# Layer 0's softmax sums: from a spread matmul and four wide reciprocals to a round trip through DRAM

## The chip, the cores and the metric

The kernel runs on one core of a Trainium2 chip, as one launch. The metric is the device time of that launch in microseconds (us); three runs of the kernel before gave 4754.49 to 4755.42 us, with a median of 4754.79 us.

## What is computed

Two attention layers run one after the other on `x` of shape (2, 256, 64, 64): two images, 256 channels, 4096 positions each. Layer 0, cut to what matters here:

```python
# xn: x normalised over its channels; q, k, v: 4 heads of 16 each
attn = softmax(einsum('bhnd,bhmd->bhnm', q, k) * SCALE, axis=-1)
d1   = relu(conv1_w @ x + conv1_b)
dyn  = conv2_w @ d1 + conv2_b            # one number for each position n
attn = attn * dyn[:, :, :, None]
out  = einsum('bhnm,bhmd->bhnd', attn, v)
x    = sigmoid(gamma * (out_w @ out) + x)
```

The kernel does not divide the 4096x4096 weights of a head by their sum. It gathers the unnormalised exponentials times v, and the sum of the exponentials beside it, and multiplies the gathered result by dyn / sum at the end. That factor, one number for each head and position, is what the change is about. Layer 1 is an ordinary attention of 4 heads of 64 with a projection and a residual; the change does not touch its code.

## The kernel before, in words

**Units and steps.** Layer 0's attention is cut into 16 units, one for each image and block of 512 query positions (`units0`). A unit runs 32 steps (`NM`), one for each 128 key positions. In every step and for each of the 4 heads, `weigh` makes the scores of those 128 keys against the 512 queries on TensorE (L440) and their exponentials on ScalarE (L443). One step later `gather` adds exponentials times v into one PSUM bank (L455): each head has a strip of 32 rows, and the first row of the strip is the sum of the exponentials, because the first column of v is one.

A second stream runs beside this and about one unit ahead (`LEAD0`, 35 steps): `maxima` makes scores of a later unit on TensorE (L402), and VectorE takes their maximum over the keys (L406), for the shift of the exponentials. A step is made of two halves, and each half emits on TensorE two score matmuls, two matmuls for maxima, and half of a gather (columns 0 to 255, then 256 to 511).

**Around the end of a unit.** When the last gather of a unit is done, ScalarE copies its bank to SBUF (`avs`, L469). What follows is hung into the steps of the next unit by `at(step, place, ...)`. With t0 the first step of the unit and NM = 32:

- `sums` at t0+33 "end": a matmul with the 0/1 matrix `spread` (L482) repeats each head's sum row over the 32 rows of its strip, in one of four PSUM banks that it shares with the maxima;
- `keep_sums` at t0+34 "start": ScalarE copies that bank to the tile `f` (L488);
- `invert` at t0+35 to t0+38 "middle": VectorE inverts `f` in four pieces of 128 columns (L492), the same number 32 times over;
- `scale` at t0+38 "end": GpSimd multiplies `f` by `dyn`, which was loaded with every row the same (L477), and then `avs` by `f` (L496, L497);
- `project` at t0+41 and t0+43 "end": TensorE multiplies by the output weights, 128 channels at a time (L502); `add_x` half a step later on VectorE adds the residual (L507);
- `finish` at t0+45 "end": a tanh on ScalarE (L516), a scaling on GpSimd (L517), and the store of the layer's output `x1` (L518).

**What sets the order.** Compute instructions are wrapped in `seq`, so that each engine runs them in the order in which the code emits them. DMAs are not: nearly all of them go to SyncE's queue (SP), and the framework places them in it, often well before the step that emits them. That queue is worked off in order, and a DMA that waits holds up what stands behind it. PSUM tiles rotate: the maxima, sums, projections and shifts share four banks (`bank`), the scores have three (`ps2`), the gather one (`psa`). A matmul waits until the earlier reader of its bank is done.

**The last unit.** From 35 steps before the end no maxima are left. The last unit runs beside layer 1's first projections (L618, L651) and the loads of their inputs, and part of its scores goes to the four shared banks.

Of the kernel before, what the change touches and what calls it, by code (L numbers as in the profile page):

```python
# [8 lines left out]
F32 = mybir.dt.float32  # L9
BF16 = mybir.dt.bfloat16  # L10
AF = mybir.ActivationFunctionType
ALU = mybir.AluOpType
# [3 lines left out]
P = 128  # L16
NB = 512
C = 256
CC = C // P
H = 4  # L20
# [7 lines left out]
def conv_attention_kernel(  # L28
# [19 lines left out]
    nc = tc.nc  # L48
    B, _, N = x.shape
    NJ = N // NB  # L50
    NM = N // P
    PB = NB // P

    const = ctx.enter_context(tc.tile_pool(name="const", bufs=1))
    dram = ctx.enter_context(tc.tile_pool(name="dram", bufs=1, space=bass.MemoryType.DRAM))
    small = ctx.enter_context(tc.tile_pool(name="small", bufs=2))
# [6 lines left out]
    l0w = own0.enter_context(tc.tile_pool(name="l0w", bufs=2))  # L63
# [11 lines left out]
    dyn0 = [  # L75
        [dram.tile([1, NB], F32, tag=f"dyn0_{b}_{j}", name=f"dyn0_{b}_{j}") for j in range(NJ)]
        for b in range(B)
    ]
    x1 = [
        [dram.tile([C, NB], F32, tag=f"x1_{b}_{j}", name=f"x1_{b}_{j}") for j in range(NJ)]  # L80
        for b in range(B)
# [4 lines left out]
    def load_x(b, j, pool=xpool, tag="x"):  # L86
        t = pool.tile([P, CC, NB], F32, tag=tag, name=f"{tag}_{b}_{j}")
        nc.sync.dma_start(
            out=t, in_=x[b, :, bass.ts(j, NB)].rearrange("(c p) n -> p c n", p=P)
        )  # L90
        return t
# [120 lines left out]
    seq = tc.keep_in_program_order  # L212
# [3 lines left out]
    def at(t, place, step):  # L216
        extras.setdefault((t, place), []).append(step)
# [13 lines left out]
    units0 = [(b, j) for b in range(B) for j in range(NJ)]  # L231
# [5 lines left out]
    with own0:  # L237
# [14 lines left out]
        work, qs0, mxs, pts, avs, dyns, res, facts = {}, {}, {}, {}, {}, {}, {}, {}  # L252

        def bank(name):
            return banks[0].tile([P, NB], F32, tag="bank", name=name)
# [129 lines left out]
        def load_q(u):  # L385
            b, j = u
            if u not in qs0:
                q = l0w.tile([P, NB], F32, tag="q", bufs=4, name=f"q_{b}_{j}")
                nc.sync.dma_start(out=q, in_=q0[b][j])
                qs0[u] = q  # L390
# [17 lines left out]
        def fold(u):  # L408
            seq(nc.vector.tensor_reduce(
                negmax0[u[1] % 2].rearrange("p i (h e) -> p (i h) e", e=32)[:, :, 0],  # L410
                mxs.pop(u), AX.X, ALU.max, negate=True,
            ))

        def turn(u):

            ps = bank("nm0_{}_{}".format(*u))
            for i in range(PB):
                seq(nc.tensor.matmul(
                    ps[:, bass.ts(i, P)], negmax0[u[1] % 2][:, i, :], ident,
                    start=True, stop=True,  # L420
                ))
            work["turn"] = ps

        def shift_q(u):
            seq(nc.vector.tensor_add(qs0[u], qs0[u], work.pop("turn")))
# [47 lines left out]
        def load_residual(u):  # L473
            b, j = u
            res[u] = load_x(b, j, res_pool, "res")
            dyns[u] = l0w.tile([P, NB], F32, tag="dyn", bufs=1, name=f"dyn_{b}_{j}")
            nc.sync.dma_start(out=dyns[u], in_=dyn0[b][j].partition_broadcast(P))  # L477

        def sums(u):
            b, j = u  # L480
            ps = bank(f"sums0_{b}_{j}")
            seq(nc.tensor.matmul(ps, spread, avs[u], start=True, stop=True))  # L482
            f = l0w.tile([P, NB], F32, tag="f", bufs=1, name=f"f0_{b}_{j}")
            facts[u] = f, ps

        def keep_sums(u):
            f, ps = facts[u]
            seq(nc.scalar.copy(f, ps))  # L488

        def invert(u, i):  # L490
            f, _ = facts[u]
            seq(nc.vector.reciprocal(f[:, bass.ts(i, P)], f[:, bass.ts(i, P)]))  # L492

        def scale(u):
            f, _ = facts.pop(u)
            seq(nc.gpsimd.tensor_tensor(f, f, dyns.pop(u), ALU.mult))  # L496
            seq(nc.gpsimd.tensor_tensor(avs[u], avs[u], f, ALU.mult))  # L497

        def project(u, c):
            b, j = u  # L500
            ps = bank(f"o0_{b}_{j}_{c}")
            seq(nc.tensor.matmul(ps, wo0[:, bass.ts(c, P)], avs[u], start=True, stop=True))  # L502
            work["o", c] = ps

        def add_x(u, c):
            xt = res[u]
            seq(nc.vector.scalar_tensor_tensor(  # L507
                xt[:, c, :], work.pop(("o", c)), gam, xt[:, c, :], ALU.mult, ALU.add
            ))

        def finish(u):
            b, j = u
            avs.pop(u)
            xt = res.pop(u)

            seq(nc.scalar.activation(xt, xt, AF.Tanh, scale=0.5))  # L516
            seq(nc.gpsimd.tensor_scalar(xt, xt, 0.5, 0.5, ALU.mult, ALU.add))  # L517
            nc.sync.dma_start(out=x1[b][j].rearrange("(c p) n -> p c n", p=P), in_=xt)  # L518


        for n, u in enumerate(units0):
            t0 = n * NM
            at(t0 - LEAD0 - 8, "start", lambda u=u: load_q(u))
            at(t0 - 4, "end", lambda u=u: fold(u))
            at(t0 - 3, "end", lambda u=u: turn(u))
            at(t0 - 2, "start", lambda u=u: shift_q(u))
            at(t0 + 12, "start", lambda u=u: load_residual(u))
            at(t0 + NM + 1, "end", lambda u=u: sums(u))
            at(t0 + NM + 2, "start", lambda u=u: keep_sums(u))
            for i in range(PB):  # L530
                at(t0 + NM + 3 + i, "middle", lambda u=u, i=i: invert(u, i))
            at(t0 + NM + 6, "end", lambda u=u: scale(u))
            for c in range(CC):
                at(t0 + NM + 9 + 2 * c, "end", lambda u=u, c=c: project(u, c))
                at(t0 + NM + 10 + 2 * c, "start", lambda u=u, c=c: add_x(u, c))
            at(t0 + NM + 13, "end", lambda u=u: finish(u))


        blocks = [(b, j) for b in range(B) for j in range(NJ)]
        for n in range(len(blocks) + 3):  # L540

            def block(k):
                return blocks[n - k] if 0 <= n - k < len(blocks) else None
# [7 lines left out]
            new, middle, old = block(0), block(1), block(2)  # L551
# [116 lines left out]
        for i in range(NJ):  # L668
            k = (0, 0, i)
            t1 = T0 + 2 + 2 * i  # L670
# [3 lines left out]
            t1 = T0 + 20 + 3 * i if i < PB else END0 + (2, 3, 4, 9)[i - PB]  # L674
# [49 lines left out]
    with (  # L724
# [330 lines left out]
        for n, u in enumerate(units):  # L1055
            b, g, j = u
            t0 = n * US
# [5 lines left out]
            if n < len(units) - NJ:  # L1063
# [9 lines left out]
                t1 = (n // NJ * NJ + NJ - 1) * US  # L1073
                at(t1 + 2 * j + 2, "start", lambda to=to: load_keys(*to))
                at(t1 + 2 * j + 3 + LAG, "start", lambda to=to: load_values(*to))
            for k in range(NG):
                t1 = t0 + (k + 1) * GS // 2
# [6 lines left out]
            t1 = t0 + US + GS // 2  # L1084
# [8 lines left out]
            if b < B - 1 and (g, j) == (PR - 1, NJ - 1):  # L1093
                for i in range(NJ):
                    t1 = t0 + US + (i + 4) * GS // 2
# [99 lines left out]
        for j in range(NJ):  # L1195
            project_half(j, 1, last_att[0][:, bass.ts(j, NB)])
            nc.sync.dma_start(
                out=out[B - 1, :, bass.ts(j, NB)].rearrange("(c p) n -> p c n", p=P),
                in_=last_x[j],
# [51 lines left out]
```

## Time and profile before

| | |
|---|---|
| median of three runs | 4754.79 us |
| the profiled execution's own time | 4754.21 us |
| its span | 4752.1 us |
| TensorE busy (matmuls) | 4539.4 us, 96% of the span |
| VectorE busy | 3957.7 us, 83% |
| ScalarE busy | 3399.4 us, 72% |
| GpSimd busy | 2554.3 us, 54% |
| the 16 units' results are copied (L469) | first at 343 us, last at 2057 us |
| from one such copy to the next | 115.66 us in the regular units, 95.6 us in the last |

The profile is one execution. A busy share is the share of the span in which an engine had an instruction in flight; an engine at 96% need not set the time everywhere, and an engine at 70% may do so where another waits for it. Layer 0's attention ends at about 2070 us; the rest is layer 1.

### The profile page before, as it was taken

How to read it: one execution, taken by the hardware profiler on the slowest of the kernel's cores; microseconds unless marked ns; L12 is line 12 of the kernel's file. 1: busy time of each engine (PE TensorE's matmuls, PEld its weight loads, DVE VectorE, ACT ScalarE, POOL GpSimd, SP SyncE). 2: the span in 40 equal slices, each digit the busy share in tenths (PEclk: the TensorE clock that was granted, in tenths of full speed). 3: DMA queues.
4: the chain of work that ended last, by engine and by line, in shares of the span. 5: the costliest groups of instructions: out<-in, count | busy, mean ns of one | idle time of the engine just before them, and what ended most of it. 6: DMA issues, size and time to landing. Idle time of an engine off the chain costs nothing.

```text
span 4752.1 us, 70463 instructions
## 1 busy us (share of the span) xinstructions
PE 4539.4 (96%) x27536; PEld 1497.5 (32%) x27536; DVE 3957.7 (83%) x4629; ACT 3399.4 (72%) x4523; POOL 2554.3 (54%) x1491
## 2 busy tenths in 40 slices
PE   8999999999999999989999999999999999999998
PEld 3433333333333333333223232323233332222222
DVE  6777777777777777459999999999999899999996
ACT  3366666666666666668888888888887778888884
POOL 5300000000000000029999999999998889999994
PEclk9999999999999999999999999999999999999999
DMA  3100000000000000110000110001111111000002
GB/s 101 35 4 19 19 19 17 15 15 14 15 15 15 14 12 17 53 61 25 16 25 23 52 32 23 25 23 36 52 33 47 62 51 45 21 14 7 14 16 73
DMA packets 105337, 139.57 MB, mean 29 GB/s; under 512 B 43884, under 2 KB 44716, under 8 KB 104892
## 3 DMA queue, kind: packets, MB, share of 16 engines
q1 hardware_dynamic: 103220, 134.61, 9.1%
q8 instruction: 216, 3.54, 0.3%
q14 instruction: 117, 0.96, 0.1%
q10 hardware_dynamic: 1784, 0.46, 0.0%
HBM read 93.33 MB, written 41.45 MB: 28 GB/s over the span
## 4 chain that ended last, share of the span: by engine, by line
PE 57%; POOL 15%; DVE 14%; issue 7%; ACT 6%; DMA 1%; SPq 0%; ACTq 0%; DVEq 0%; POOLq 0%
PE s L440 23%; POOL acc L914 13%; PE av L455 12%; DVE rmax L824 9%; PE s L807 6%; PE av L924 5%; DVE raw L890 4%; ACT raw L825 4%; PE a L402 2%; POOL acc L912 1%; PE p L262 1%; ACT raw L902 1%; PE k1p L618 1%; PE rt L832 1%; PE o L502 1%
## 5 line engine op out<-in xcount | busy, mean ns | idle before, releaser
L914 POOL TENSOR_TENSOR acc<-acc,raw 128x1024 f32<-128x1024 f32 x884 | 2097.0, 2372 | 90.8 <-ACT raw L902 31.2
L406 DVE TENSOR_REDUCE mx<-a 128x1 f32<-128x512 f32 x2048 | 1311.6, 684 | 422.5 <-PE a L402 421.3
L443 ACT ACTIVATE p<-s 128x512 f32<-128x512 f32 x2048 | 1108.2, 595 | 697.6 <-PE a L402 350.6
L807 PE MATMUL s<-q,k 64*128 64x512 f32 x4096 | 1116.9, 636 | 143.7 <-ACT raw L825 135.1
L890 DVE TENSOR_TENSOR raw<-raw,shift 128x1024 f32<-128x1024 f32 x1024 | 1236.8, 1212 | 19.5 <-PE shift L885 13.6
L824 DVE TENSOR_TENSOR rmax<-s,rmax 128x1024 f32<-128x1024 f32 x960 | 1169.1, 1218 | 72.6 <-PE s L807 70.7
L825 ACT COPY raw<-s 128x1024 f32<-128x1024 f32 x1024 | 1036.9, 1013 | 260.6 <-DVE rmax L824 170.0
L440 PE MATMUL s<-q,kT 32*128 32x512 f32 x4096 | 1215.3, 640 | 0.0
L902 ACT ACTIVATE raw<-raw 128x1024 f32<-128x1024 f32 x1024 | 1085.3, 1060 | 179.4 <-DVE raw L890 147.9
L402 PE MATMUL a<-kT,q 32*128 32x512 f32 x4096 | 1128.3, 642 | 1.8 <-DVE mx L406 1.6
L924 PE MATMUL av<-raw,v 128*64 128x512 f32 x4096 | 999.3, 606 | 2.0
L496 POOL TENSOR_TENSOR f<-f,dyn 128x512 f32<-128x512 f32 x16 | 20.2, 1266 | 1434.1 <-ACT p L443 1377.8
L455 PE MATMUL av<-p,v 128*32 128x256 f32 (+1 forms) x7904 | 650.1, 399 | 0.6 <-ACT avs L469 0.6
L807 PEld LDWEIGHTS s<-q,k 64*128 64x128 f32 x4096 | 316.9, 185 | 828.5 <-ACT raw L825 629.5
L440 PEld LDWEIGHTS s<-q,kT 32*128 32x128 f32 x4096 | 394.2, 183 | 430.2 <-issue 385.7
L924 PEld LDWEIGHTS av<-raw,v 128*64 128x64 f32 x4096 | 243.2, 136 | 587.7 <-issue 429.4
L455 PEld LDWEIGHTS av<-p,v 128*32 128x32 f32 x7904 | 157.6, 108 | 751.5 <-issue 737.2
L402 PEld LDWEIGHTS a<-kT,q 32*128 32x128 f32 x4096 | 304.4, 183 | 31.9 <-DVE mx L406 18.9
L517 POOL TENSOR_SCALAR res<-res 128x1024 f32<-128x1024 f32 x16 | 16.7, 1044 | 379.7 <-ACT res L516 379.7
L912 POOL TENSOR_TENSOR acc<-raw,raw 128x1024 f32<-128x1024 f32 x64 | 152.3, 2380 | 113.0 <-ACT raw L902 104.1
L844 DVE TENSOR_REDUCE negs<-rt 128x4 f32<-128x512 f32 x128 | 88.2, 689 | 50.2 <-PE rt L832 47.8
L310 DVE RECIPROCAL std<-std 128x128 f32<-128x128 f32 x64 | 56.1, 920 | 39.2 <-ACT std L305 39.2
(329 smaller groups left out, 1924.0 us busy)
## 6 DMA issues: line engine op xcount, KB each, us to landing
x<-in_x_dram SPq DMA_DIRECT2D x16, 512.0 KB
res<-in_x_dram SPq DMA_DIRECT2D x16, 512.0 KB
x<-res SPq DMA_DIRECT2D x16, 512.0 KB
att<-rows SPq DMA_DIRECT2D x62, 128.0 KB
kd<-k1s SPq DMA_DIRECT2D x24, 256.0 KB
vd<-v1s SPq DMA_DIRECT2D x24, 256.0 KB
k<-kd SPq DMA_DIRECT2D x24, 256.0 KB
v<-vd SPq DMA_DIRECT2D x24, 256.0 KB
```

Of the source, the lines that this page charges most:

```text
L402: seq(nc.tensor.matmul(ps, qs0[u][r, bass.ts(i, P)], kTs[b][r, bass.ts(m, NB)], start=True, stop=True,))
L406: seq(nc.vector.tensor_reduce(mxs[u][:, i * H + h, m : m + 1], ps, AX.X, ALU.max))
L440: seq(nc.tensor.matmul(ps, kTs[b][r, bass.ts(m, P)], qs0[u][r, :], start=True, stop=True))
L443: seq(nc.scalar.activation(pt[:, k, :], ps, AF.Exp, scale=D0**-0.5))
L455: seq(nc.tensor.matmul(avs[u][32 * h : 32 * h + 32, cols], vs0[b][:, m, 32 * h : 32 * h + 32], pts[t, h // 2][:, h % 2, cols], start=(m == ...
L807: seq(nc.tensor.matmul(ps[:, k, :], ks[b, g, m // PB][r, bass.ts(m % PB, P)], qs1[u][r, :], start=True, stop=True,))
L824: seq(nc.vector.tensor_tensor(rmax[u, n], ps, before, ALU.max))
L825: seq(nc.scalar.copy(raw, ps))
L890: seq(nc.vector.tensor_tensor(raws[t], raws[t], shifts[u, t % NM // GS], ALU.add))
L902: seq(nc.scalar.activation(p, p, AF.Exp, scale=D1**-0.5))
L914: seq(nc.gpsimd.tensor_tensor(accs[u, n], accs[u, n], p, ALU.add))
L924: seq(nc.tensor.matmul(avs1[u, n][k * D1 : (k + 1) * D1, :], v[:, m % PB, k, :], raws[t][:, k, :], start=(m % GS == 0), stop=(m % GS == GS ...
```

## The change

For the first 15 of the 16 units the spread matmul, its copy and the four wide reciprocals go. The four sum rows of `avs` (one for each head, 512 numbers) are stored to DRAM by four DMAs, and read back as 128 partitions with 16 numbers each; VectorE inverts this small tile once, GpSimd multiplies it by `dyn` in the same layout, and it is stored to DRAM as a factor. Four more DMAs read it back, each row of a head repeated over 32 partitions, and GpSimd multiplies `avs` by it. `dyn` itself is loaded in the layout of 16 to a partition, by four DMAs in place of one. The projections, additions and the finish of such a unit come six steps later than before. The last unit is left as it was.

```diff
+    sum0, fac0 = (
+        [
+            [dram.tile([H, NB], F32, tag=f"{s}_{b}_{j}", name=f"{s}_{b}_{j}") for j in range(NJ)]
+            for b in range(B)
+        ]
+        for s in ("sum0", "fac0")
+    )
...
             res[u] = load_x(b, j, res_pool, "res")
-            dyns[u] = l0w.tile([P, NB], F32, tag="dyn", bufs=1, name=f"dyn_{b}_{j}")
-            nc.sync.dma_start(out=dyns[u], in_=dyn0[b][j].partition_broadcast(P))
+            if u == units0[-1]:
+                dyns[u] = l0w.tile([P, NB], F32, tag="dyn", bufs=1, name=f"dyn_{b}_{j}")
+                nc.sync.dma_start(out=dyns[u], in_=dyn0[b][j].partition_broadcast(P))
+                return
+            dyns[u] = small.tile([P, NB // 32], F32, tag="dyn16", name=f"dyn_{b}_{j}")
+            for h in range(H):
+                nc.sync.dma_start(
+                    out=dyns[u][32 * h : 32 * h + 32, :],
+                    in_=dyn0[b][j].rearrange("o (r c) -> (o r) c", c=NB // 32),
+                )
+
+        by_row = "h (r c) -> (h r) c"
+
+        def send_sums(u):
+            b, j = u
+            for h in range(H):
+                nc.sync.dma_start(
+                    out=sum0[b][j][h : h + 1, :], in_=avs[u][32 * h : 32 * h + 1, :]
+                )
+            f = small.tile([P, NB // 32], F32, tag="f16", name=f"f16_{b}_{j}")
+            nc.sync.dma_start(out=f, in_=sum0[b][j].rearrange(by_row, c=NB // 32))
+            facts[u] = f
+
+        def factor(u):
+            b, j = u
+            f = facts.pop(u)
+            seq(nc.vector.reciprocal(f, f))
+            seq(nc.gpsimd.tensor_tensor(f, f, dyns.pop(u), ALU.mult))
+            nc.sync.dma_start(out=fac0[b][j].rearrange(by_row, c=NB // 32), in_=f)
+            f = l0w.tile([P, NB], F32, tag="f", bufs=1, name=f"f0_{b}_{j}")
+            for h in range(H):
+                nc.sync.dma_start(
+                    out=f[32 * h : 32 * h + 32, :],
+                    in_=fac0[b][j][h : h + 1, :].partition_broadcast(32),
+                )
+            facts[u] = f
+
+        def scale_all(u):
+            seq(nc.gpsimd.tensor_tensor(avs[u], avs[u], facts.pop(u), ALU.mult))
...
-            at(t0 + NM + 1, "end", lambda u=u: sums(u))
-            at(t0 + NM + 2, "start", lambda u=u: keep_sums(u))
-            for i in range(PB):
-                at(t0 + NM + 3 + i, "middle", lambda u=u, i=i: invert(u, i))
-            at(t0 + NM + 6, "end", lambda u=u: scale(u))
+            if u == units0[-1]:
+                t1 = t0 + NM + 9
+                at(t0 + NM + 1, "end", lambda u=u: sums(u))
+                at(t0 + NM + 2, "start", lambda u=u: keep_sums(u))
+                for i in range(PB):
+                    at(t0 + NM + 3 + i, "middle", lambda u=u, i=i: invert(u, i))
+                at(t0 + NM + 6, "end", lambda u=u: scale(u))
+            else:
+                t1 = t0 + NM + 15
+                at(t0 + NM + 1, "start", lambda u=u: send_sums(u))
+                at(t0 + NM + 6, "start", lambda u=u: factor(u))
+                at(t0 + NM + 12, "start", lambda u=u: scale_all(u))
             for c in range(CC):
-                at(t0 + NM + 9 + 2 * c, "end", lambda u=u, c=c: project(u, c))
-                at(t0 + NM + 10 + 2 * c, "start", lambda u=u, c=c: add_x(u, c))
-            at(t0 + NM + 13, "end", lambda u=u: finish(u))
+                at(t1 + 2 * c, "end", lambda u=u, c=c: project(u, c))
+                at(t1 + 1 + 2 * c, "start", lambda u=u, c=c: add_x(u, c))
+            at(t1 + 4, "end", lambda u=u: finish(u))
```

## The prediction, made before the changed kernel ran

> **What bounds the kernel now.** I read first the forty slices of the page, then the busy times of one regular unit of layer 0 (345 to 461 us), then the timeline of each engine around the end of a unit.
>
> ```profile
> PE   8999999999999999989999999999999999999998
> DVE  6777777777777777459999999999999899999996
> ACT  3366666666666666668888888888887778888884
> ```
>
> The change lives in slices 3 to 17. There TensorE is at nine tenths, VectorE at seven, ScalarE at six. The busy times of one unit (columns: stretch, sum, then PE, PEld, DVE, ACT, POOL) say the same:
>
> ```profile
> 345.00:461.00 116.00, 116.00 (x1042) 38.42 (x1038) 87.86 (x137) 71.46 (x132) 3.58 (x3) 1.00 0.06 19
> ```
>
> Read alone, the 87.86 us of VectorE say that relieving it buys nothing, and TensorE without a gap says that each matmul taken away pays in full. The second is not quite so, which TensorE's timeline shows. Each half step begins its gather at L455:
>
> ```profile
> 799.99 0.64 PE L455 MATMUL av<-p,v 128*32 128x256 f32 x8
> ...
> 801.73 0.64 PE L455 MATMUL av<-p,v 128*32 128x256 f32 x8
> ...
> 803.49 0.64 PE L455 MATMUL av<-p,v 128*32 128x256 f32 x8
> ...
> 806.99 0.64 PE L455 MATMUL av<-p,v 128*32 128x256 f32 x8
> ...
> 808.63 0.64 PE L455 MATMUL av<-p,v 128*32 128x256 f32 x8
> 809.20 1.12 PE L482 MATMUL sums<-avs,spread 128*128 128x512 f32 x2
> 810.26 0.70 PE L440 MATMUL s<-q,kT 32*128 32x512 f32 x2
> ...
> 811.33 0.64 PE L455 MATMUL av<-p,v 128*32 128x256 f32 x8
> ```
>
> 799.99 to 803.49 is one step: 3.50 us, in halves of 1.74 and 1.76. I followed these starts through a whole unit: the halves are 1.74+1.76, 1.80+1.70, 1.68+1.82 or 1.64+1.86, but each step that holds nothing else takes 3.50. TensorE's own work in a half is only 1.64 (the 1.64 halves). The other 0.22 us of a step is a wait for ScalarE: the second score of a half needs a bank whose exponential is just being read (three score banks, two scores in a half). What a half loses so, the next has back, so the sum stays at 3.50. The step with the spread matmul, 806.99 to 811.33, takes 4.34: 0.84 more, though the matmul holds TensorE for 1.06 (809.20 to 810.26). The rest, 0.22, is the wait for ScalarE, which the matmul hides. So **0.84 us** is what a unit can win.
>
> VectorE, in the steps in which it inverts:
>
> ```profile
> 818.47 1.29 DVE L406 TENSOR_REDUCE mx<-a 128x1 f32<-128x512 f32 x2 [0.22 <-PE a L402]
> 819.67 0.94 DVE L492 RECIPROCAL f<-f 128x128 f32<-128x128 f32 x1
> 820.53 1.22 DVE L406 TENSOR_REDUCE mx<-a 128x1 f32<-128x512 f32 x2
> 821.97 1.29 DVE L406 TENSOR_REDUCE mx<-a 128x1 f32<-128x512 f32 x2 [0.22 <-PE a L402]
> ```
>
> It waits for TensorE only 0.22 us in such a step, but it does wait, and these steps still take 3.50 (1.64+1.86). The inversions are hidden, just.
>
> **What the Trainium skill says.** "TensorE: Matmul & The Clock Gate", under "Why this matters for your kernels": a matmul of depth 32 takes as long as one of depth 128, and the gain of small ones is that several run at once. The trace agrees: a pass of a score of depth 32 (L440) lasts 640 ns in the mean, one of the spread matmul 644. So one spread matmul, which fills the array, costs as much as the eight score passes of half a step.
> "DMA: Bandwidth & Descriptors", "Anatomy of one DMA": about 2.0 us fixed for a DMA, and a wait stands on the issuing queue. Agrees: SP stores a block of q at 66.62 and issues its load, which waits for the store, at 68.61, 1.99 us; the q load issued at 801.82 (256 KB) has landed at 804.42.
> The same page, "Specifications": pieces under 512 B do not reach line rate. The new 16-number rows are pieces of 64 B; no transfer of this kind stands near the change in the trace of before.
>
> **The change part by part.**
> *Removed from TensorE:* 15 spread matmuls. Fourteen lie in regular units, 14 x 0.84 = 11.8 us. The fifteenth (unit 14's) lies in the last unit, without maxima. There the step with it and a key projection runs from the gather at 1961.73 to that at 1966.57, 4.84 us; a step with a key projection alone from 1975.75 to 1979.73, 3.98: 0.86 us. Bounds: nothing, if ScalarE with its 0.54 us an exponential takes over, to the full 1.06.
> *Removed from ScalarE:* 15 copies of 586 ns (L488). Steps with it take 3.50 like the others: hidden, 0. If a gain, at most the 0.22 us wait, once a unit.
> *Removed from VectorE:* 60 reciprocals of 940 ns (L492). Hidden under TensorE as shown: 0. Were that cover gone it would be 3.8 us a unit.
> *Removed from GpSimd:* 15 multiplications of 1266 ns (L496), which nobody waited for: 0.
> *Added to VectorE:* 15 reciprocals of 128x16. The nearest row is layer 1's 128x8 at 203 ns (L984); the 128x128 one has (940-203)/120 = 6 ns a column more, so about 0.25 us: hidden, since it lies in steps that lose up to 0.94.
> *Added to GpSimd:* 15 products of 128x16; 128x8 takes 206 ns (L985). 0.
> *Added wait 1:* the reciprocal waits for the sums' round trip. Behind it in VectorE's queue stand the maxima, which free TensorE's banks. In the unit of the timeline the copy of `avs` ends at 806.84 (806.25 + 0.59). Four stores at 0.29 us of SP each (1.15 for the four stores of dyn rows at 61.12) are issued by 808.0, landed about 2 later, 810.0; the load of 64 B pieces is issued 0.33 later and lands in 2 to 6 us (2.6 is the 256 KB load above; the upper end doubles that for the small pieces and rounds up), 812.4 to 816.4. The reciprocal is emitted at t0+38 "start", half a step before the last inversion (826.67), so at about 824.9. Spare: 8 to 12 us. Cost 0.
> *Added wait 2:* `scale_all` on GpSimd waits for the factor. Reciprocal, product, store and four loads: 0.25 + 0.2 + 2.0 + 4 x 0.33 + 3.0 (the landing of the 256 KB dyn load issued at 1981.81) = 6.8 us, against six steps, 21 us. Behind it stand only the unit's own later steps; the projection comes 3.5 steps later. Cost 0.
> *Moved:* projections, additions, tanh and x1's store, six steps later. The two projections of before cost 0.84 and 0.94 (steps of 4.34 and 4.44), the tanh's step 0.06. Between the turn of the maxima (t0+29) and the first projection the halves settle at 1.64+1.86 within four steps, and keep it. They meet the moved projections in the same phase, with the same distances to each other: 0.
> *SP's queue:* in the build's order sum stores, small load, factor store, dyn loads, factor loads, x1 store, residual load, q load follow each other. What stands behind the new waits is due later anyhow: the q load waits for its buffer until the next unit's end. In the last unit the key load k6 stands behind the factor loads. It was issued at 1978.76 and is now issued at about 1984, and its matmul runs at 1997: 0. The x1 store moves behind three value loads, which wait for buffers, not for it.
> *PSUM:* the four banks rotate without the sums. In the last unit, I worked the rotation out: the bank waits on VectorE stay the same except that those behind the projections move with them, each with another matmul of 2 us between. 0.
>
> Sum: 11.8 + 0.86 = 12.6 us. Against the profiled execution: 4754.21 - 12.6 = 4741.6; the median stands 0.58 above it, so **4742.2 us**. Layer 1's instructions keep their order, so I add nothing there.
>
> **Rivals.**
> *Full price:* each matmul pays 1.06 and the saved copy gives ScalarE's 0.22 back as well: 15 x 1.06 = 15.9, so 4738.9. For it: TensorE shows no gap. Against: the 4.34 of the step.
> *Out of phase:* the moved projections meet longer halves, and each pays its whole 1.06: 15 x (0.22 + 0.12) = 5.1 back, 4747.3, within the noise of no change. Against: the pattern is the same in all regular units.
> *The round trip is late (slower):* the small load has not landed when VectorE reaches the reciprocal; the maxima stop, TensorE's banks run full, and each us beyond the spare is paid in each unit. It decides from (12.6 + 9.5) / 15 = 1.5 us beyond the spare, a load of 64 B pieces of 12 us or more. With 3 us beyond: 4754.8 - 12.6 + 45 = 4787. For it: VectorE has only 0.2 us of slack in a crowded step, so it cannot hide a stop. Against: all landings I read took 2 to 3 us.
>
> **How the numbers follow.** Forecast 0.78 (own range 4740.5 to 4745), full price 0.07, out of phase 0.10, late 0.05. 0.2% is 9.5 us, about what a measurement of this kernel tells from no change. Faster by more: 0.78 + 0.07 = 0.85; within: 0.10; slower: 0.05. The range 4738.5 to 4746.5 holds the first two and the edge of the third.
>
> **What would show it.** In the profile after: regular units of 114.82 us from copy to copy in place of 115.66; the step at t0+33 at 3.50; steps with projections still 4.34 and 4.44, six steps later; reciprocals of 128x16 near 0.25 us, before which VectorE never waits for a DMA. A wait of the reciprocal for its load, or of TensorE for the maxima behind it, would make the prediction wrong; so would a plain step that isn't 3.50.

## The result, and the profile after

The changed kernel takes 4741.30 us in the median of nine runs (4739.79 to 4742.40), the kernel before 4754.73 us in nine (4753.31 to 4755.42): a ratio of 0.9972, with a 95% interval of 0.9964 to 0.9981. The profiled execution took 4741.58 us with a span of 4739.8, against 4754.21 and 4752.1 before: 12.6 us less in time, 12.3 in the span.

Where the 12.6 us come from, by the copies of `avs` that end the units: a regular unit now takes 114.85 us in place of 115.66, 0.81 less; so does the second last of the 15 intervals, partly without maxima (112.78 in place of 113.59); the last one takes 94.87 in place of 95.63, 0.77 less. That is 14 x 0.81 + 0.77 = 12.1. Two units in either execution were longer than the others by 0.3 to 0.6, which leaves 11.8 between the first copy and the last. The rest of the 12.6 lies before the first copy (0.2), behind the last one (0.2 to 0.3) and outside the span (0.3); I did not follow it up. One regular unit, from copy to copy:

```profile
802.50 0.59 ACT L477 COPY avs<-av 128x512 f32<-128x512 f32 x1
...
917.34 0.59 ACT L477 COPY avs<-av 128x512 f32<-128x512 f32 x1
```

The page's forty slices of TensorE, VectorE and ScalarE differ from those before in one digit, of VectorE, and show nothing of it. The busy times of a regular unit (stretch, sum, then PE, PEld, DVE, ACT, POOL) do, but only in part. In these stretches, each a unit long to within 0.4 us, VectorE has 2.6 us less to do, ScalarE 0.6, GpSimd 1.0, and TensorE is as full as before.

```profile
345.00:460.00 115.00, 115.00 (x1044) 38.31 (x1036) 85.27 (x134) 70.89 (x130) 2.54 (x3) 1.00 0.06 20
```

TensorE's timeline, from the half step in which `avs` is copied (802.50) on. The spread matmul, which stood before the last gather shown here, is gone:

```profile
801.42 0.64 PE L463 MATMUL av<-p,v 128*32 128x256 f32 x8
...
803.24 0.64 PE L463 MATMUL av<-p,v 128*32 128x256 f32 x8
...
804.88 0.64 PE L463 MATMUL av<-p,v 128*32 128x256 f32 x8
805.45 0.92 PE L448 MATMUL s<-q,kT 32*128 32x512 f32 x2
805.68 0.70 PE L410 MATMUL a<-kT,q 32*128 32x512 f32 x2
...
806.74 0.64 PE L463 MATMUL av<-p,v 128*32 128x256 f32 x8
```

803.24 to 806.74 is the step that took 4.34 us; it now takes 3.50, like any other, in halves of 1.64 and 1.86. In the longer half the matmuls for the maxima start 0.23 us after the scores, because the second score waited for its bank: the wait that the spread matmul used to hide is back. That it is this wait is shown further down, by the runs with a shortened exponential and with the banks moved. The steps with the projections, now six steps later, still take 4.34 and 4.44:

```profile
852.26 0.64 PE L463 MATMUL av<-p,v 128*32 128x256 f32 x8
...
856.60 0.64 PE L463 MATMUL av<-p,v 128*32 128x256 f32 x8
...
860.10 0.64 PE L463 MATMUL av<-p,v 128*32 128x256 f32 x8
...
864.54 0.64 PE L463 MATMUL av<-p,v 128*32 128x256 f32 x8
```

VectorE and SP around the narrow inversion:

```profile
819.06 1.29 DVE L414 TENSOR_REDUCE mx<-a 128x1 f32<-128x512 f32 x2 [0.39 <-PE a L410]
820.26 0.24 DVE L512 RECIPROCAL f<-f 128x16 f32<-128x16 f32 x1
820.88 1.29 DVE L414 TENSOR_REDUCE mx<-a 128x1 f32<-128x512 f32 x2 [0.38 <-PE a L410]
```

```profile
803.12 1.12 SPq L502 DMA_DIRECT2D sum<-avs  x4
805.21 0.35 SPq L506 DMA_DIRECT2D f<-sum  x1
820.84 0.34 SPq L514 DMA_DIRECT2D fac<-f  x1
821.22 3.01 SPq L490 DMA_DIRECT2D dyn<-dyn  x4
824.28 1.81 SPq L517 DMA_DIRECT2D f<-fac  x4
```

The inversion waits for nothing: the small load, issued at 805.21, has landed at 806.82 (the last of the 16 increments of its semaphore in the trace), and VectorE comes to it at 820.26.

### The profile page after: what moved, and what is told of

Same layout as the page of the kernel before. It is cut to its first block, busy times and chain, and to the rows that moved or that the text cites. A ratio compares the mean times of both kernels' runs of the same rounds, so it can differ in the third digit from the quotient of the medians.

```text
span 4739.8 us, 70643 instructions
## 1 busy us (share of the span) xinstructions
PE 4526.9 (96%) x27506; PEld 1496.2 (32%) x27506; DVE 3917.0 (83%) x4584; ACT 3394.1 (72%) x4508; POOL 2540.6 (54%) x1491
## 4 chain that ended last, share of the span: by engine, by line
PE 58%; DVE 15%; POOL 15%; issue 6%; ACT 5%; DMA 1%; SPq 0%; ACTq 0%; DVEq 0%; POOLq 0%
PE s L448 24%; POOL acc L968 13%; PE av L463 12%; DVE rmax L878 10%; PE s L861 6%; PE av L978 5%; DVE raw L944 4%; ACT raw L879 4%; PE a L410 2%; PE p L270 1%; PE k1p L672 1%; POOL acc L966 1%; PE rt L886 1%; PE q1p L672 1%; PE o L549 1%
```

## The experiments

My theory was that the change is worth what TensorE's spread matmul cost, which is its 1.06 us less a wait for ScalarE that it hid. The rivals were VectorE's relief, ScalarE's copy, the matmul's full price, and, on the other side, a late round trip. Times are medians; a ratio is to runs of the kernel before on the same chip.

**The matmul alone put back** into the changed kernel:

```diff
+        def spare_sums(u):
...
+            ps = bank(f"sums0_{b}_{j}")
+            seq(nc.tensor.matmul(ps, spread, avs[u], start=True, stop=True))
...
+                at(t0 + NM + 1, "end", lambda u=u: spare_sums(u))
```

> The changed kernel, with the spread matmul put back at its old place in the first 15 units; nothing reads what it makes, and no copy or wide reciprocal follows. If TensorE's matmul is what the change saved, at 0.81 to 0.84 us a unit, nearly all of the gain is gone: about 4754 us, regular units of 115.66 us, the step with the matmul 4.34 us. If VectorE's reciprocals or ScalarE's copy made the gain, it stays: 4741 to 4742 us, units of 114.85. If part of it was theirs, the time lies between, and the unit's length says how much.

Measured: 4755.17 us, ratio 1.0001 (0.9993 to 1.0009). Regular units take 115.66 us, and the step with the matmul is back, though nothing of VectorE's or ScalarE's old work is:

```profile
806.55 0.64 PE L463 MATMUL av<-p,v 128*32 128x256 f32 x8
...
808.19 0.64 PE L463 MATMUL av<-p,v 128*32 128x256 f32 x8
808.76 1.13 PE L549 MATMUL sums<-avs,spread 128*128 128x512 f32 x2
...
810.89 0.64 PE L463 MATMUL av<-p,v 128*32 128x256 f32 x8
```

806.55 to 810.89 is 4.34. One matmul a unit, whose result nobody reads, takes the whole gain away.

**ScalarE's copy alone put back.** It reads from SBUF what the old one read from the matmul's bank:

```diff
+        def spare_copy(u):
...
+            f = l0w.tile([P, NB], F32, tag="spare", bufs=1, name=f"spare_{b}_{j}")
+            seq(nc.scalar.copy(f, avs[u]))
...
+                at(t0 + NM + 2, "start", lambda u=u: spare_copy(u))
```

> The changed kernel, with a copy of 128x512 by ScalarE put back at the place of the old one (from SBUF into a tile that nothing reads), without the matmul. If the copy was hidden, nothing changes: 4741 to 4742 us, units of 114.85 us. If ScalarE's 0.59 us counted because TensorE waits for its exponentials in every second half step, a unit becomes up to 0.22 us longer, 15 x 0.22 = 3 us: about 4744.5; at its full price 15 x 0.59 = 9 us: 4750.

Measured: 4741.08 us, ratio 0.9969 (0.9957 to 0.9982): the copy was hidden. Units take 114.76 us, 0.09 less than without it; one plain step beside it takes 3.44. The copy did no harm, and why a unit is shorter by these hundredths I did not settle.

**VectorE's work alone taken from the kernel before** (the columns beyond the 16th stay uninverted):

```diff
+            if u != units0[-1]:
+                if i == PB - 1:
+                    seq(nc.vector.reciprocal(f[:, :16], f[:, :16]))
+                return
```

> The kernel before, in which the first 15 units invert only 16 columns, once, in place of four times 128; the other columns stay uninverted, so part of the division is left out. Matmul, copy and all places stay. If VectorE's work was hidden, nothing changes: 4754 to 4755 us, units of 115.66. If VectorE, with 0.2 us of slack in those steps, set the pace there, up to 4 x 0.2 us a unit are won: down to 4743 us.

Measured: 4755.87 us, ratio 1.0002 (0.9994 to 1.0010), units of 115.66 us. Its groups of reciprocals show that 15 narrow ones stand in the place of 60 wide ones (the four left are the last unit's):

```profile
L494 DVE RECIPROCAL f<-f 128x16 f32<-128x16 f32 x15 | 3.6, 243 | 0.0
```

The four wide reciprocals, the largest item in the unit's busy times that the change removes, were worth nothing.

**The matmul and its copy replaced by DRAM, the wide reciprocals kept.** What follows in such a unit, from the reciprocals on, stands four steps later; the edits for this and for the last unit are left out here:

```diff
-            seq(nc.tensor.matmul(ps, spread, avs[u], start=True, stop=True))
...
+            for h in range(H):
+                nc.sync.dma_start(
+                    out=sum0[b][j][h : h + 1, :], in_=avs[u][32 * h : 32 * h + 1, :]
+                )
+            for h in range(H):
+                nc.sync.dma_start(
+                    out=f[32 * h : 32 * h + 32, :],
+                    in_=sum0[b][j][h : h + 1, :].partition_broadcast(32),
+                )
...
```

> The kernel before, in which the first 15 units spread their sums by DRAM (four stores, four loads repeated over 32 partitions) in place of the matmul and its copy, and keep all else: four reciprocals of 128 columns a unit, and the wide product with dyn. They and the projections stand four steps later than before. If TensorE's matmul is the whole gain, this has it too: 4741 to 4743 us, units of 114.85. If the narrow inversion counts as well, the time lies between 4742 and 4754, and the steps that invert are longer than 3.50 us.

Measured: 4741.46 us, ratio 0.9973 (0.9962 to 0.9984), units of 114.82 us. Half of the change, without the layout of 16 to a partition, has all of its gain. Its group of reciprocals shows that VectorE still did all of them:

```profile
L508 DVE RECIPROCAL f<-f 128x128 f32<-128x128 f32 x64 | 59.8, 940 | 14.8 <-ACT f L504 14.8
```

**Why 0.84 and not 1.06.** In two kernels ScalarE's first exponential of each pair is cut from 512 to 192 columns, so that its bank comes free sooner; GpSimd fills the rest with ones:

```diff
+                if k == 0:
+                    seq(nc.gpsimd.memset(pt[:, k, 192:], 1.0))
+                    seq(nc.scalar.activation(
+                        pt[:, k, :192], ps[:, :192], AF.Exp, scale=D0**-0.5
+                    ))
+                    continue
```

In the kernel before:

> The kernel before, in which ScalarE takes the exponential of only 192 of 512 columns for the first of each pair of heads (GpSimd fills the rest with ones), so part of the weights is left out. If the 0.22 us that a plain step takes beyond TensorE's own work is a wait for this exponential, plain steps fall from 3.50 to 3.28 us, a unit to about 109 us, and the time by some 95 us to about 4660. If something else holds the step at 3.50 (VectorE's maxima, the issue of matmuls), it stays there.

In the changed kernel:

> The same shortening of ScalarE's first exponentials, in the changed kernel. If the spread matmul was worth 0.84 and not 1.06 us because it hid the wait for ScalarE, then without that wait the change is worth the full price: units 1.06 us shorter than those of the kernel before with the same shortening, 14 x 1.06 + 0.9 = 15.7 us in all. If 0.84 is the matmul's own price, the two differ by 12.6 us as before.

Measured: 4656.87 and 4640.35 us, ratios of 0.9793 (0.9780 to 0.9806) and 0.9758 (0.9745 to 0.9772). Plain steps are 3.28 us in both, and the step with the spread matmul is the same 4.34 as ever (the first of the two):

```profile
802.29 0.64 PE L461 MATMUL av<-p,v 128*32 128x256 f32 x8
...
803.93 0.64 PE L461 MATMUL av<-p,v 128*32 128x256 f32 x8
...
806.63 0.64 PE L461 MATMUL av<-p,v 128*32 128x256 f32 x8
...
808.27 0.64 PE L461 MATMUL av<-p,v 128*32 128x256 f32 x8
```

Between these gathers lie 1.64, 2.70 and 1.64 us. Most regular units take 109.29 us in the one and 108.23 or 108.24 in the other (some are 0.2 to 0.5 longer in both): the same change is now worth 1.06 a unit, and 16.5 us in all, where 15.7 were expected. The matmul's price is its duration; 0.22 of it is lost where ScalarE makes TensorE wait anyway.

**The phase of the projections:**

```diff
-                at(t1 + 2 * c, "end", lambda u=u, c=c: project(u, c))
...
+                gap = 2 if u in units0[-2:] else 5
+                at(t1 + gap * c, "end", lambda u=u, c=c: project(u, c))
...
```

> The changed kernel, with the two projections of the first 14 units five steps apart in place of two. If the second one's step takes 4.44 and not 4.34 us because it meets the halves before they have settled at 1.64 and 1.86, it now takes 4.34, and a unit is 0.10 shorter: 114.75 us, 1.4 us in all, about 4740. If the 0.10 comes from the addition on VectorE beside it, the step stays at 4.44.

Measured: 4739.04 us, ratio 0.9967 (0.9954 to 0.9979), units of 114.72 us, 0.13 less than in the changed kernel. Both steps with a projection now take 4.34. The 0.10 us by which the second one was longer was the phase, not the addition. This is the fastest version of the full computation here, but it cannot be told from the changed kernel by its time.

**A round trip that is late.** First, the inversion 4.5 steps earlier:

```diff
-                at(t0 + NM + 6, "start", lambda u=u: factor(u))
+                at(t0 + NM + 1, "end", lambda u=u: factor(u))
```

> The changed kernel, with the narrow inversion emitted at t0+33 end in place of t0+38 start, 4.5 steps earlier. In the changed kernel's trace the small load lands 13.4 us before the reciprocal; 4.5 steps are 15.7 us, so the reciprocal reaches its place about 2.3 us too early, waits for the load, and the maxima behind it wait too. If the late round trip costs as the slower rival says, each us is paid once the two maxima banks in reserve are used up (0.4 to 1.5 us): 15 x 0.8 to 15 x 2.1 = 12 to 31 us, 4753 to 4772. If VectorE can catch up, since it idles 0.4 us in each half step, nothing: 4741 to 4742.

Measured: 4740.93 us, ratio 0.9971 (0.9960 to 0.9982), units of 114.82 us.

```profile
805.06 1.29 DVE L414 TENSOR_REDUCE mx<-a 128x1 f32<-128x512 f32 x2 [0.39 <-PE a L410]
807.09 0.25 DVE L512 RECIPROCAL f<-f 128x16 f32<-128x16 f32 x1 [0.74 <-issue]
807.25 2.59 DVE L414 TENSOR_REDUCE mx<-a 128x1 f32<-128x512 f32 x4
```

VectorE did wait, 0.74 us here and 0.4 to 1.0 in the other units that have maxima, and made up for it: four maxima follow without a gap. But I had placed it wrongly: the inversion comes after the maxima of its step, and so was late by 0.7 us and not by 2.3. The run did not test the price, so I made the trip longer, with the inversion as early as in this run:

```diff
+            for again in range(2):
+                d = dram.tile([H, NB], F32, tag=f"more{again}_{b}_{j}", name=f"more{again}_{b}_{j}")
+                nc.sync.dma_start(out=d.rearrange(by_row, c=NB // 32), in_=f)
+                f = small.tile([P, NB // 32], F32, tag=f"f16{again}", name=f"f16{again}_{b}_{j}")
+                nc.sync.dma_start(out=f, in_=d.rearrange(by_row, c=NB // 32))
```

> The run with the early factor, in which the sums go through DRAM twice more before they are inverted (a store and a load of the 128x16 tile each time). In the run with the early factor the load landed about 0.7 us after VectorE was ready, at no cost. In the changed kernel a store and a load take some 1.7 us each, so two more trips make it about 7 us later, 7.7 in all. If VectorE and the maxima banks absorb only what they have in reserve (about 0.5 us of idle time and 0.9 us between the end of a maximum and the need for its bank), a unit pays some 6.3 us: 15 x 6.3 = 95 us, about 4836 us (range 4810 to 4850), and TensorE's matmuls for the maxima wait for VectorE. If the wait is made good later, since VectorE idles 0.4 us in each half step, it stays near 4741.

Measured: 4861.38 us, ratio 1.0222 (1.0207 to 1.0237), units of 122.4 to 123.7 us, about 8 us more than in the changed kernel. That is above the 4810 to 4850 us that I had expected. VectorE and then TensorE in one unit:

```profile
837.32 1.29 DVE L414 TENSOR_REDUCE mx<-a 128x1 f32<-128x512 f32 x2 [0.39 <-PE a L410]
845.95 0.25 DVE L517 RECIPROCAL f<-f 128x16 f32<-128x16 f32 x1 [7.34 <-DMA f<-more]
```

```profile
841.22 1.35 PE L448 MATMUL s<-q,kT 32*128 32x512 f32 x4
846.80 2.66 PE L410 MATMUL a<-kT,q 32*128 32x512 f32 x4 [4.24 <-DVE mx L414]
849.40 1.08 PE L463 MATMUL av<-p,v 128*32 128x256 f32 x8
```

The wait is where the slower rival put it: VectorE stands before the inversion, the maxima stand behind it in VectorE's queue, and TensorE's matmul for the maxima waits for VectorE. It costs more than its length: 8 us for a wait of 7.3. The gather at 849.40 lasts 1.08 us in place of 0.64, and the granted clock (the number after the five engines) says why:

```profile
834.00:841.00 7.00, 7.00 (x72) 2.28 (x64) 3.69 (x6) 4.82 (x10) 0.00 (x0) 1.00 0.04 6
841.00:848.00 7.00, 2.76 (x15) 1.51 (x8) 2.05 (x5) 1.97 (x4) 0.22 (x1) 0.82 0.05 5
848.00:855.00 7.00, 7.00 (x48) 1.73 (x48) 3.70 (x6) 1.95 (x4) 1.27 (x1) 0.69 0.15 39
```

**The bank moved from the maxima to the scores:**

```diff
...
-        ps1 = own_psum.enter_context(tc.tile_pool(name="ps1", bufs=4, space=PSUM))
-        ps2 = own_psum.enter_context(tc.tile_pool(name="ps2", bufs=3, space=PSUM))
+        ps1 = own_psum.enter_context(tc.tile_pool(name="ps1", bufs=3, space=PSUM))
+        ps2 = own_psum.enter_context(tc.tile_pool(name="ps2", bufs=4, space=PSUM))
```

In the last unit three of seven scores, and not four, go to the shared banks.

> The changed kernel, with four banks for the scores and three for the maxima in place of three and four. The wait of the second score for ScalarE's exponential goes. With three banks the second maximum of a half waits for VectorE's first one of the half before in the same way: VectorE's 684 ns are 0.09 longer than the exponential's 595, so a plain step should take 3.55 to 3.6 us in place of 3.50, and the time rise by 25 to 45 us, to 4766 to 4786. If VectorE, which starts a maximum as soon as it is made, keeps clear of the wait, steps fall to 3.28 and the time to about 4645.

Measured: 4805.53 us, ratio 1.0105 (1.0088 to 1.0122). A plain step takes 3.61 us, in halves of 1.97 and 1.64:

```profile
800.52 0.64 PE L463 MATMUL av<-p,v 128*32 128x256 f32 x8
801.09 0.70 PE L448 MATMUL s<-q,kT 32*128 32x512 f32 x2
801.10 1.03 PE L410 MATMUL a<-kT,q 32*128 32x512 f32 x2
...
802.49 0.64 PE L463 MATMUL av<-p,v 128*32 128x256 f32 x8
...
804.13 0.64 PE L463 MATMUL av<-p,v 128*32 128x256 f32 x8
```

In the longer half it is now the matmuls for the maxima that are held up (1.03 us in place of 0.70), and no longer the scores: the wait has gone over to the maxima, and is longer there, as expected in kind. The time rose by 64 us over the changed kernel, more than my 25 to 45; the step was 0.11 longer, not 0.05 to 0.10, the projections then cost 1.05 each, and 8 us of the 64 lie before the first copy of `avs` (351.1 us in place of 343.1), which I had left out.

## Why the prediction was right, point by point

*What bounds layer 0.* Right. A plain step is TensorE's 3.28 us and a wait of 0.22 for ScalarE's exponential; with the exponential cut short exactly 3.28 is left.

*The price of the matmul, 0.84 us in a regular unit.* Right: the step fell from 4.34 to 3.50, and the unit by 0.81 in the changed kernel's profile and by 0.84 in the two variants with units of 114.82. Where the changed kernel's units lose the 0.03 is open. The full price, the first rival, is ruled out for this kernel, and shown to hold once the wait is gone.

*Unit 14's matmul, 0.86.* The step itself, from the gather at 1950.43 to that at 1954.41, now takes 3.98 in place of 4.84: just the 0.86. The last interval as a whole became 0.77 shorter.

*Reciprocals and copy at nothing.* Right, each shown by a run of its own. The inversions were the tempting reading: the change takes four inversions of 0.94 us out of a unit and is described by them, and VectorE had only 0.2 us of slack in the steps that inverted. But it had that slack, and hence they cost nothing.

*The waits.* Right that they cost nothing, wrong in size. I gave the small load 2 to 6 us; it took 1.6 (805.21 to 806.82), so VectorE had 13.4 us to spare and not 8 to 12. `scale_all` is not held to its step either: GpSimd has nothing in front of it and multiplies when the factor has landed, at 827.87, 7.6 us after the inversion where the prediction's sum was 6.8.

*The moved projections at nothing.* Right: 4.34 and 4.44 as before. The second rival's phase is a real thing, as the run with the projections apart shows, but it is worth 0.10 us.

*SP's queue.* Right that it costs nothing, wrong on the way there: the key load k6 was to be issued some 5 us later, behind the factor loads. Counted from the gather that begins the step with unit 14's spread matmul, it was issued after 17.0 us before (1961.73 to 1978.76) and after 16.2 now (1950.43 to 1966.61).

*The slower rival.* Its mechanism and place were right, its price of one us for each us was not: waits of 0.4 to 1.0 us came free, and the one of 7.3 us cost TensorE's clock as well. The point from which this rival was to decide is added up wrongly, too. From the load's issue at 810.3 to the reciprocal at 824.9 are 14.6 us, and with 1.5 beyond it the load would have to take some 16 us, not 12.

*The sum.* 12.6 us predicted against the profiled execution, 12.6 found; 4742.2 us predicted for the median, 4741.3 found, with runs that scatter by up to 1.5 us to either side. That the first two agree to a tenth is luck: all 12.6 were put between the copies of `avs`, where 11.8 were found, and the other 0.8 lies where the prediction had nothing.

## What to carry to other kernels

Take the price of a removed instruction from the step that holds it against a step that doesn't, not from its duration: here 1.06 us of matmul were worth 0.84, because a wait moved into the gap. The engine whose load a change lightens most need not be the one that pays; put single parts back, and one run for each tells. The round trip through DRAM was free here because VectorE, which keeps the order of the code, comes to it 13 us after it has landed; up to 1 us of waiting for it was made up for, and 7 us of waiting cost 8.

## What was not expected of the hardware

- DMAs of 16 numbers (64 B) a piece were quick. In the run with two more trips a store of the 128x16 tile was issued at 839.05 and the load that waits for it at 840.47, 1.4 us later; the next store at 842.72, 2.3 us after that load was issued. "DMA: Bandwidth & Descriptors", in the Trainium skill, "Specifications", has pieces below 512 B fall short of line rate; here the 8 KB landed no later than the load of 256 KB, which the prediction read at 2.6 us. No run moves the same 8 KB in larger pieces, so what the small pieces cost is not shown.
- A row of DMAs can hold SP for longer than its single issues suggest. The issues of the `dyn` and factor loads take 0.42 us in the median, and most rows of eight take 3.7 us; the row from 821.22 to 826.09 takes 4.9, because one of its issues takes 1.61. Two other rows of the changed kernel have such a long issue, of 1.45 and 1.54 us, most have none, and what makes it long is open.
- TensorE, stopped for 4.2 us in the run with two more trips (842.57 to 846.80), came back at half its clock: the clock's records have it at half from 845.50 to 852.32, 6.8 us, and as long in twelve other units. The Trainium skill, "TensorE: Matmul & The Clock Gate", under "Why this matters for your kernels", warns of such a drop after idle gaps of more than some 3 us; this agrees.
